# When the first x tile of the layers is loaded: at the start of the kernel, or when the first Gram matrix has been turned

## The chip, the cores and the metric

The kernel runs on one core of one Trainium2 chip. The metric is the time on the device, in microseconds (us), of one execution of the whole program; lower is better. Everything is in 32-bit floats.

## What is computed

x has the shape (16, 32, 128, 128). Two layers follow each other, each as x + layer(group norm of x).

```python
# layer 0: linear attention over channels, 8 images of 32 channels at a time
q = _proj(xf, Wq); kv = _proj(xf, Wkv); k, v = kv[:, :inner], kv[:, inner:]
sim = jnp.einsum('bin,bjn->bij', qh, kh) * scale
attn = jax.nn.softmax(sim, axis=-1)
out = _proj(jnp.einsum('bnj,bjd->bnd', attn, vh), Wout, bout)
# layer 1: windows of 8 x 8, layer norm, then four "fastkan" maps
#   fastkan(t) = exp(-((ln(t) - GRID) / DENOM) ** 2) @ ws.T + silu(t) @ wb.T + bb
z = fastkan1(rows) + fastkan2(columns) + fastkan3(channels)
out = fastkan4(z) + wins
# the whole
x = x + _L0_conv_ref(_gn(x), ...)
x = x + _L1_conv_ref(_gn(x), ...)
```

Layer 0 is linear in x apart from a small matrix that depends on x only through its second moments. The kernel uses this: for each half of the batch (8 images, 256 rows of 16384 values) it forms the 256 x 256 Gram matrix of x, works out from it one small matrix (`pts`) that stands for the normalisation and the attention together, and then applies that matrix to x while layer 1 runs.

## The kernel before

**Two stages.** The first goes once over all of x for the two Gram matrices. The second goes over x again in 64 units (one unit is 128 rows by 1024 columns; two units share one loaded tile `x` of 128 x 2 x 1024 values, 1 MB) and does everything else.

**The Gram stage.** Three tasks pass data along.

- `gram_load` (line 690) fetches x in 16 steps, m = 0 to 15, 2 MB each, eight to a Gram matrix: four DMAs of 256 KB from SP's queue and four from ACT's. The tiles are borrowed from the layers. For m < 8 there are three pairs in turn, (`ad`, `yy`), (`u`, `u`) and (`d`, `sd`); from m = 8 on only the first two, since `d` and `sd` are given back when the first matrix is turned. Step m waits until the last step with its pair has been turned: `"turned", 4 * old[-1] + 3`.
- `gram_turn` (line 711) transposes one block of 512 columns at a time on DVE, four blocks to a step, 32 blocks (`STEPS`) to a matrix, and announces each with `put(("turned", m), None)`. Its two buffers `R` allow it to be two blocks ahead of PE.
- `gram_sum` (line 737) multiplies each turned block with itself on PE and adds up in a PSUM tile `X`.

`attention(bp)` follows each matrix: a long chain of small steps between PE, DVE and ACT that begins with copies of the Gram matrix (the one on ACT is line 799) and ends with `pts[bp]`. `projections` and `parameters` fetch and prepare weights through POOL's queue.

**The first steps of the layers.** `load(n)` (line 1057) fetches `x` for units n and n + 1 with eight DMAs of 128 KB from SP's queue; the pool holds one `x` tile. `layer0_norm(n)` (line 1067) multiplies it with `pts`, so it needs `x` and `attention`. After it come `keep`, `centre`, `rows_norm`, `move`, `norm_a` and the rest of layer 1.

**What sets the order.** Every task is a Python generator that yields steps, each with an engine, an assumed duration and the tiles it takes, or asks for something with `yield "get", key`. A planner (`Flow.run`) runs them against a clock of its own when the program is built, and the order in which it lets steps go is the order of the instructions on each engine. Nothing of its clock reaches the chip; there an instruction waits only for data and for free tiles. The text `ORDER` fixes the order of all named layer tasks on each engine. On SP `load` of unit 0 is the first of them. Until the second Gram matrix is found, only unit 0 holds others back; tasks that are not named, like `gram_load`, fit in where they are not late against a named step that is ready:

```python
late = c[0] > at or (c[0] == at and unit < AHEAD and name not in FIRST)
```

The planner's assumed durations that matter here: `load` 5.2 us of SP; a step of `gram_load` 2.6 us of SP and then 2.6 us of ACT; a sum 0.57 us for a quarter of a block; `parameters` 85 us of POOL, for its many small DMAs.

Of the kernel before, what the change touches and what calls it, by code (L numbers as in the profile page):

```python
# [88 lines left out]
def step(engine, us, *take, lag=None):  # L89


    return engine, us, take, LAG if lag is None else lag


class Flow:
# [22 lines left out]
    def put(self, key, value, late=0.0):  # L118
        self.found[key] = (value, self.now + late)
# [134 lines left out]
def conv_preact_kernel(  # L254
# [248 lines left out]
    def layers():  # L503
        with ExitStack() as es:
# [157 lines left out]
            STEPS = S // 512  # L662
# [385 lines left out]
            def load(n):  # L1048

                if n % 2:  # L1050
                    return
                bp, kk, j = units[n]
                xr, = yield step("SP", 5.2, "x")
                for k in range(KK):
                    for b in range(4):
                        o = slice(32 * b, 32 * b + 32)
                        nc.sync.dma_start(out=xr[o, k, :], in_=x_raw[bp, o, k, j * RB : (j + 1) * RB])
                put(("x", n // 2), xr, fl.moved(2.6, 4.5))
# [509 lines left out]
            with tc.manual_schedule(engines=IN_ORDER):  # L1568
# [25 lines left out]
                        every("assist", assist),  # L1594
                        every("layer0_norm", layer0_norm),
                        every("load", load),
                        every("store", store),
                        ((f"ladder_{k}", n, ladder(k, n)) for k, n in both),
# [85 lines left out]
```

## Time and profile before

| what | value |
|---|---|
| three runs | 2644.55, 2648.94, 2655.05 us; median 2648.94 |
| the profiled execution | 2646.42 us; span in the profile 2644.5 us |
| busy PE, DVE, ACT, POOL | 95%, 93%, 87%, 27% of the span |
| mean granted clock of PE | 0.988 |
| Gram stage: first block turned, first sum of the second matrix, last sum | 17.75, 98.60, about 210.9 us |
| the layers in full swing | from about 244 us |

How to read it: PE is the matrix engine (PEld its weight loads), DVE the vector engine, ACT the scalar engine, SP the engine that mostly issues DMAs. A line of the timeline gives start, length, engine, source line, operation, result <- operand, count, and in brackets the idle time of the engine before it and what ended that. "SPq" and "ACTq" are DMAs being issued; a line with x8 runs from the first issue to the last. A line of windows gives the stretch, its length, the busy time of PE, PEld, DVE, ACT and POOL with the number of instructions, the clock granted to PE (1.00 is full), the mean busy share of the 16 DMA engines, and GB/s (reads and writes as the DMA engines moved them).

### The profile page before, as it was taken

Reading aid. Unit: us, or ns where it says so; the run is one execution under the profiler, and the core shown is the slowest. Engines: PE = TensorE matmul, PEld = TensorE weight load, DVE = VectorE, ACT = ScalarE, POOL = GpSimd, SP = SyncE. Lnnn points to the kernel's source line nnn. Section 1 sums busy time; section 2 is a strip of 40 time slices with the busy share of each in tenths; the row PEclk is TensorE's granted clock in tenths of the full one; section 3 lists DMA queues with packets and bytes.
Section 4 is the critical chain, followed back from the end, with each engine's and each line's share of the span. In section 5 each row is a group of like instructions: output and inputs, shape, how many; then the busy total and the mean of one; then the engine's idle time right before and its main releaser. Section 6 shows DMA issues by size and latency. Waiting matters only on the chain.

```text
span 2644.5 us, 126397 instructions
## 1 busy us (share of the span) xinstructions
PE 2505.3 (95%) x57375; PEld 1300.0 (49%) x57375; DVE 2460.2 (93%) x1697; ACT 2306.0 (87%) x1969; POOL 704.8 (27%) x559
## 2 busy tenths in 40 slices
PE   6998999999999999999999999999999999999875
PEld 6884544444444444444444444444444444444431
DVE  4755899999999999999999999999999999999977
ACT  0007699999999999999999999999999999999973
POOL 4301132232222332232332222322223322323300
PEclk9998999999999999999999999999999999999998
DMA  9752345555555555555555555555555555555521
GB/s 245 193 152 65 106 118 151 147 145 152 144 147 151 155 144 149 145 148 155 145 146 156 139 147 155 153 146 146 147 146 156 142 146 149 146 149 158 140 74 45
DMA packets 306613, 379.86 MB, mean 144 GB/s; under 512 B 42912, under 2 KB 240032, under 8 KB 306080
## 3 DMA queue, kind: packets, MB, share of 16 engines
q1 hardware_dynamic: 292728, 352.22, 48.8%
q10 hardware_dynamic: 9640, 17.11, 2.5%
q8 instruction: 453, 7.42, 1.2%
q0 software_dynamic: 3712, 2.46, 0.4%
q14 instruction: 80, 0.66, 0.1%
HBM read 103.18 MB, written 67.11 MB: 64 GB/s over the span
## 4 chain that ended last, share of the span: by engine, by line
PE 51%; DVE 12%; DMA 10%; ACT 9%; issue 7%; POOL 5%; SPq 5%; DVEq 0%; ACTq 0%; POOLq 0%
PE X L480 25%; DVE u L1276 9%; POOL att L1291 5%; PE X L500 5%; PE Y L1035 4%; DMA out<-xh 4%; PE Y L480 4%; PE X L737 3%; ACT R L1248 3%; PE Y L1213 3%; ACT u L1245 2%; PE Y L1067 2%; ACT z L1389 2%; PE Y L1128 2%; PE X L1477 2%
## 5 line engine op out<-in xcount | busy, mean ns | idle before, releaser
L1276 DVE SCALAR_TENSOR_TENSOR u<-R,u 128x2048 f32<-128x2048 f32 x781 | 1818.4, 2352 | 39.1 <-ACT u L1257 9.7
L480 PE MATMUL X<-u,wt_a 32*32 32x512 f32 x16384 | 666.6, 600 | 12.0 <-ACT u L1257 8.6
L480 PE MATMUL X<-u,wt_b 32*32 32x512 f32 x16896 | 601.4, 600 | 14.3 <-DVE u L1276 12.8
L480 PEld LDWEIGHTS X<-u,wt_a 32*32 32x32 f32 x16384 | 318.1, 103 | 226.2 <-issue 126.3
L1291 POOL TENSOR_SCALAR att<-R 128x1024 f32<-128x1024 f32 x64 | 278.4, 4350 | 548.3 <-ACT R L1248 548.3
L1245 ACT ACTIVATE u<-yc,vec 128x2048 f32<-128x2048 f32 x195 | 391.1, 2006 | 31.0 <-DVE yc L1230 16.1
L1257 ACT ACTIVATE u<-u 128x2048 f32<-128x2048 f32 x195 | 371.0, 1903 | 2.1
L1230 DVE TENSOR_TENSOR yc<-yc,Y 128x1024 f32<-128x1024 f32 x260 | 310.0, 1212 | 18.1 <-PE Y L1213 17.7
L480 PEld LDWEIGHTS X<-u,wt_b 32*32 32x32 f32 x16896 | 206.5, 103 | 237.6 <-issue 104.2
L1320 POOL MEMSET vec<- 128x1 f32 x130 | 12.8, 98 | 1138.9 <-PE X L500 1136.9
L1204 ACT ACTIVATE yc<-Y 128x1024 f32<-128x1024 f32 x260 | 250.0, 1012 | 39.3 <-PE Y L480 38.7
L1248 ACT ACTIVATE R<-yc,vec 128x2048 f32<-128x2048 f32 x130 | 259.6, 1997 | 0.0
L1207 ACT ACTIVATE u<-yc 128x2048 f32<-128x2048 f32 x130 | 247.4, 1904 | 2.2
L1067 PE MATMUL Y<-x,pt 128*128 128x512 f32 x512 | 238.5, 609 | 0.0
L737 PE MATMUL X<-R 128*64 128x193 f32 (+3 forms) x2048 | 153.1, 310 | 24.8 <-DVE R L711 24.3
L1067 PEld LDWEIGHTS Y<-x,pt 128*128 128x128 f32 x512 | 92.9, 191 | 144.4 <-issue 141.0
L737 PEld LDWEIGHTS X<-R 128*64 128x64 f32 x2048 | 142.2, 141 | 39.1 <-DVE R L711 26.3
L1296 POOL TENSOR_TENSOR u<-att,u 128x1024 f32<-128x1024 f32 x64 | 151.9, 2374 | 2.6 <-DVE u L1276 1.4
L1143 POOL TENSOR_SCALAR yy<-yy,vec,col_r 128x1024 f32<-128x1024 f32 x64 | 111.8, 1747 | 147.7 <-DVE yy L1139 125.9
L1366 ACT ACTIVATE ad<-X,col 128x1024 f32<-128x1024 f32 x128 | 135.7, 1120 | 0.8 <-PE X L480 0.6
L500 PE MATMUL X<-sd,ws_a 32*32 32x512 f32 x2048 | 95.8, 598 | 33.3 <-ACT z L1389 18.4
L480 PE MATMUL Y<-yy,c 32*32 32x512 f32 x1056 | 125.2, 598 | 0.4 <-ACT yc L1204 0.4
(222 smaller groups left out, 2929.9 us busy)
## 6 DMA issues: line engine op xcount, KB each, us to landing
xh<-xh SPq DMA_DIRECT2D x512, 128.0 KB
d<-yy SPq DMA_DIRECT2D x512, 128.0 KB
sd<-S SPq DMA_DIRECT2D x512, 128.0 KB
ad_r<-ad SPq DMA_DIRECT2D x512, 128.0 KB
x<-in_x SPq DMA_DIRECT2D x256, 128.0 KB
out<-xh SPq DMA_DIRECT2D x508, 64.0 KB
u<-in_x SPq DMA_DIRECT2D x28, 256.0 KB
u<-in_x ACTq DMA_DIRECT2D x28, 256.0 KB
```

What stands on the lines that cost most here:

```text
L480: MM(dst(to, g_), lhsT=wt[32 * g_ : 32 * g_ + 32, :], rhs=rhs(g_, to ^ cross[g_]), start=start, stop=stop,)
L500: done.append(MM(dst(g_ ^ w, q), lhsT=wt[o, q // 2, :], rhs=rhs(o, q), start=start, stop=stop))
L737: MM(g[64 * q : 64 * q + 64, k, lo:hi], lhsT=t[:, b, at : at + 64], rhs=t[:, b, lo:hi], start=first, stop=last,)
L1067: MM(xp[:, u, :], lhsT=pts[bp][:, k, kk * P : (kk + 1) * P], rhs=xr[:, k, u * 512 : (u + 1) * 512], start=k == 0, stop=k == KK - 1,)
L1204: ACT(v[:, i * RB : (i + 1) * RB], flat(yt[i]), AF.Identity)
L1207: ACT(sq, v, AF.Square)
L1230: TT(v[:, o], v[:, o], flat(rb[i]), ALU.mult)
L1245: ACT(u, v, AF.Square, bias=bqs[k])
L1248: ACT(up, v, AF.Exp, bias=bp_, scale=2.0)
L1257: ACT(u, u, AF.Exp, scale=-1.0, bias=lift)
L1276: STT(t, by, BIG, at, ALU.min, ALU.mult)
L1291: nc.gpsimd.tensor_scalar(rc, by[:, 0:RB], BIG, None, ALU.min)
```

## The change

`load(0)` first asks for `("turned", STEPS - 1)`, the key that `gram_turn` puts when block 31, the last of the first Gram matrix, has been turned. `load` returns at once for odd units, so the one tile concerned is the one for units 0 and 1. No DMA is added, removed or resized, and the loads for later units ask for nothing new.

```diff
                 if n % 2:
                     return
                 bp, kk, j = units[n]
+                if n == 0:
+                    yield "get", ("turned", STEPS - 1)
                 xr, = yield step("SP", 5.2, "x")
                 for k in range(KK):
                     for b in range(4):
```

## The prediction

> **What bounds the kernel now.** The page comes first. After the third of its 40 slices (66 us each) PE, DVE and ACT are all full, and nothing that the change touches lies there. The first slice is the one with a PE of 6 tenths and a DMA of 9.
>
> ```profile
> PE   6998999999999999999999999999999999999875
> PEclk9998999999999999999999999999999999999998
> DMA  9752345555555555555555555555555555555521
> ```
>
> Second, the chain of waits in the first 150 us: start, length, what held.
>
> ```profile
> 0.72 2.65 DMA x<-in_x
> 3.40 6.64 DMA x<-in_x
> 10.05 7.68 DMA ad<-in_x
> 17.75 10.36 DMA u<-in_x
> 28.14 8.25 DMA sd<-in_x
> 36.41 10.78 DMA yy<-in_x
> 47.20 12.93 DMA u<-in_x
> ...
> 61.08 34.80 PE X L737 x358
> ```
>
> Up to 60.3 us only arrivals count, and the first 9.3 us are named x, a tile that nothing reads until much later. From 61.08 the Gram matmuls (L737) carry the chain. Third, the timeline, for the instructions that matter: the x load, the first turned block, the loads of steps m = 8 (ad, yy) and m = 9 (u), the first reader of m = 9, the first reader of x.
>
> ```profile
> 0.72 7.61 SPq L1057 DMA_DIRECT2D x<-in_x  x8
> 17.75 0.71 DVE L711 STREAM_TRANSPOSE R<-ad 128x512 f32<-128x512 f32 x1 [9.17 <-DMA ad<-in_x]
> 61.08 19.20 PE L737 MATMUL X<-R 128*64 128x257 f32 x251 [3.66 <-DVE R L711]
> 87.47 0.42 SPq L690 DMA_DIRECT2D yy<-in_x  x1
> 94.44 2.46 SPq L690 DMA_DIRECT2D u<-in_x  x4
> 94.45 2.48 ACTq L690 DMA_DIRECT2D u<-in_x  x4
> 108.77 1.52 DVE L711 STREAM_TRANSPOSE R<-u 128x512 f32<-128x512 f32 x2 [0.96 <-PE X L737]
> 148.01 3.60 PE L1067 MATMUL Y<-x,pt 128*128 128x512 f32 x8
> ```
>
> Block 36, the first of m = 9, is turned at 108.77 after a wait for PE, not for data. Last, windows, for the room on the DMA engines (the last two columns are the DMA share and GB/s).
>
> ```profile
> 56.00:60.00 4.00, 1.42 (x22) 1.19 (x18) 0.71 (x1) 0.00 (x0) 2.20 (x3) 1.00 1.04 296
> 84.00:86.00 2.00, 2.00 (x33) 1.88 (x31) 1.23 (x3) 0.00 (x0) 2.00 (x5) 1.00 0.08 9
> 94.00:96.00 2.00, 2.00 (x33) 1.88 (x31) 1.23 (x3) 0.00 (x0) 1.67 (x4) 1.00 0.57 145
> 102.00:104.00 2.00, 2.00 (x27) 1.67 (x27) 1.86 (x10) 0.72 (x2) 0.24 (x1) 1.00 0.70 193
> 104.00:106.00 2.00, 2.00 (x21) 1.79 (x17) 1.85 (x11) 0.00 (x0) 0.00 (x0) 1.00 0.03 8
> ```
>
> m = 9 has finished moving by about 103.4 (0.70 of the window that ends at 104), 5.4 us before its reader at 108.77.
>
> **Part 1: x leaves the head of SP's queue.** Eight DMAs of 128 KB, 1.049 MB, and 7.61 us of SP before its first Gram load at 8.38. The DMA engines are saturated (share above 1.0 in every 10 us from 10 to 80), so what is saved is the time of the bytes. Over 4 to 20 us the windows moved 228, 220, 214 and 222 GB/s, mean 221: 1.049 / 0.221 = 4.7 us, by which the first block would be turned earlier. Where the data last holds PE (61.08) the rate is 296 GB/s, because the attention's weights come in beside: 1.049 / 0.296 = 3.5 us. These are the two ends; I take the middle, 4.1 us, since both rates occur on the way.
>
> The Trainium skill ("DMA: Bandwidth & Descriptors", section on bandwidth) gives 341 GB/s for a single 1 MB load issued by GpSimd. By that figure the saving is estimated at 3.1 us. The trace's 221 GB/s, with SP and ACT both loading, disagrees.
>
> Does PE pass it on? In the windows 60 to 100, 100 to 150 and 150 to 211 us it is busy 38.48 + 49.05 + 59.67 = 147.2 of 151 us. This stretch is PE's, so an earlier start shifts its end, and all behind it, by the same amount.
>
> One reserve. PE waits 3.66 us before 61.08, and the clock granted is 0.50 in 62 to 64 and 0.66 in 64 to 66: 2 x 0.50 + 2 x 0.34 = 1.7 us lost. The wait should stay as long as it is, since both its ends move forward by 3.5 to 4.7 us; I change nothing, and keep 1.7 us each way.
>
> The Trainium skill ("TensorE: Matmul & The Clock Gate", Part 1) has the clock halve after an idle window of about 3.4 us that runs freely. By that rule a wait this near the limit may or may not cost its 1.7 us, in either version.
>
> **Part 2: where x lands.** The wait is a "get" of the planner, which only orders the program; the x tile has no earlier user, so the instruction itself should wait for nothing. The planner lets it go when block 31 is turned, the moment at which m = 9 (same block, turn 1) also becomes free. At equal times a named task of unit 0 goes first, so SP's order becomes: m = 8, x, m = 9. On the chip x then starts right behind m = 8, at 87.9 on the old clock, not at 94.4. The gap at 84 to 86 (share 0.08) can't be used, because SP stands in front of m = 8, which waits for its buffer.
>
> Behind x on SP stand four DMAs of m = 9, on which DVE (block 36) and then PE wait. The price: the idle share 0.43 x 2 = 0.9 us of 94 to 96 is filled; the rest of x pushes m = 9. At 260 GB/s (the mean of 96 to 104) x takes 4.0 us, so m = 9 ends at 103.4 + 4.0 - 0.9 = 106.5, still 2.3 us before 108.77. If SP did wait until 94.4, nothing would be filled and m = 9 would end at 107.4, still in time.
>
> ACT's half is reordered too. In the plan SP is taken 5.2 us by x, so ACT's half of m = 9 comes due 5.2 us after block 31, while attention's copy of the Gram matrix (L799) comes due after one more sum, 4 x 0.57 = 2.3 us, and hand-overs, about 3 us. The copy should go first, and it ran at 98.20, waiting for PE: ACT's four DMAs then issue at about 98.5 instead of 94.45. Their 1.05 MB need 4.0 us alone, and SP's share fills the engines before them, so the end stays near 106 to 107. I take 0 for part 2. Its ends are 0 (nothing there waits for less than before, so a gain is excluded) and the whole 4.1 us given back.
>
> x itself is read at 148.01, over 40 us after it lands: no cost. m = 10 is issued at 105.66 and read at 124.10, and takes up the last of the push.
>
> **Part 3: the order around it.** By the planner's costs the Gram starts 5.2 us earlier while "parameters" (85 us on POOL) does not move, so parameter steps slide two blocks later among the Gram's and attention's steps on DVE and PE. No row shows this; the nearest is the one wait of PE for a turned block between 84 and 130 us, 1.5 us long. One such more or less: bounds -1.5 and +1.5, I take 0, because PE is full there with either order. After the second Gram matrix the order is written out for all named tasks, and all of it shifts alike.
>
> **Sum.** -4.1 + 0 + 0 against the profiled execution: its span 2644.5, its time 2646.42, so 2642.3. That execution is 2.5 us below the median of the runs, 2648.94; on the median the forecast is 2644.8.
>
> **Rivals.** *Given back (about 2649).* x costs its 4.1 us in the second Gram instead of the first. For it: x sits right in front of m = 9, and loads there are double, not triple buffered. Against: 5.4 us of slack, and PE sums block 36 only at 113.06. It decides if m = 9 ends after 108.77, which means less than 5.24 MB / 23.1 us = 227 GB/s from 85.64 (two loads and x) on. 96 to 104 ran at 193 to 320.
>
> *Slower (about 2666).* The same lateness, but it repeats: m = 9, 11, 13 and 15 share one buffer, so m = 9 late makes the next of them late, and each late load stops PE as at 57 to 66 us, 3.7 us of wait and 1.7 us of half clock, 5.4 us. All four, 21.6, minus 4.1, give +17.5 on the profiled time, 2663.9, on the median 2666.4; three are not yet past 0.5%. It decides if m = 9 arrives more than about 4.3 us after 108.77, where PE runs out of turned blocks at 113.06, and if nothing makes the delay good. Against: the DMA share is 0.03 in 114 to 116 and 0.01 in 116 to 120, room in which a delay dies out.
>
> *Faster still (about 2639).* The wait before 61.08 and its half clock vanish besides: 4.1 + 3.7 + 1.7 = 9.5 us, on the median 2639.4; only with a run as low as the lowest shown (4.4 below the median) is that past 0.5%. For it, PE's first start gains the larger end; against, a PE that starts earlier waits longer for the same arrival.
>
> **How the numbers follow.** Forecast 0.60, given back 0.16, slower 0.12, faster still 0.12. 0.5% is 13.2 us, about what a measurement of this kernel can tell from no change (its runs span 10.5). The forecast and the given-back case lie within it, and half of faster still: 0.60 + 0.16 + 0.06 = 0.82. Faster is the other half, 0.06, slower 0.12. Range: down, 2644.8 - 1.5 (order) - 1.7 (clock) - 4.4 (lowest run against median) = 2637; up, the given-back 2649 plus 6.1 (highest run against median) = 2655. It leaves out the slower case and the lower half of the faster one.
>
> **What would show it.** Right: the first block turned at 13 to 14 us, the first Gram's last block near 91, x on SP directly behind m = 8 and before m = 9, L799 before ACT's m = 9, no DMA named as what block 36 waited for, and every later stage 3.5 to 4.7 us earlier. Part 2 is wrong if block 36 waits for u; part 1 is wrong if the first block is earlier but PE's second start at 61.08 is not; part 3 is wrong if PE stands idle in the second Gram for more than the 3.8 us of before. A difference that grows along the layers would make the whole argument wrong.

## The result, and the profile after

The changed kernel takes **2667.31 us** (median of 6 runs, 2664.78 to 2673.37) against 2648.47 us (6 runs, 2644.55 to 2657.88) of the kernel before beside it: a ratio of **1.0071, 95% interval 1.0052 to 1.0091**. It is slower by 18.8 us. The forecast was 2644.8 us and no measurable change, so the prediction was wrong. Below, "before" and "after" are the two kernels' profiled executions; the spans are 2644.5 and 2663.0 us, the mean clocks 0.988 and 0.982.

Two rows of the page after, of those that the prediction showed of before:

```profile
PE   7997999999999999999999999999999999999875
PEclk9997999999999999999999999999999999999988
```

PE's first slice rose from 6 to 7 tenths, as wanted: PE starts earlier. Its fourth slice (200 to 266 us) fell from 8 to 7, and the clock there from 8 to 7. From the fifth slice on the row of PE is the same, but a 9 stands for 90% or more and hides a loss of some us. The table below shows that the loss begins in the second Gram matrix and is not complete before the sixth product of the layers, at about 369 us.

The chain of waits after (start, length, what held):

```profile
55.33 10.68 PE X L737 x100
...
177.46 6.15 DMA d<-yy
183.67 6.26 DMA u<-in_x
```

PE's second start, at 61.08 before, is at 55.33. New are two arrivals late in the second Gram matrix, a transfer of `move(0)` (d) and, by the name that the profile gives it, a load of the last Gram step (u).

The timeline after:

```profile
11.04 0.71 DVE L711 STREAM_TRANSPOSE R<-ad 128x512 f32<-128x512 f32 x1 [1.41 <-DMA yy<-in_x]
85.09 12.31 SPq L1059 DMA_DIRECT2D x<-in_x  x8
107.96 0.71 DVE L711 STREAM_TRANSPOSE R<-u 128x512 f32<-128x512 f32 x1 [0.37 <-DMA u<-in_x]
176.12 7.13 SPq L1189 DMA_DIRECT2D d<-yy  x8
183.67 3.21 SPq L690 DMA_DIRECT2D u<-in_x  x4
189.93 2.02 PE L480 MATMUL Y<-d,c 32*32 32x512 f32 x32 [6.07 <-DMA u<-in_x]
198.50 1.52 DVE L711 STREAM_TRANSPOSE R<-u 128x512 f32<-128x512 f32 x2 [2.85 <-PE X L737]
210.42 1.17 PE L1215 MATMUL Y<-lr,back_b 32*128 32x128 f32 x32
215.37 1.21 DVE L1232 TENSOR_TENSOR yc<-yc,Y 128x1024 f32<-128x1024 f32 x1
239.94 1.21 DVE L1232 TENSOR_TENSOR yc<-yc,Y 128x1024 f32<-128x1024 f32 x1
```

And the same places in the timeline of before, which the prediction did not look at:

```profile
181.99 2.54 SPq L690 DMA_DIRECT2D u<-in_x  x4
186.43 8.54 SPq L1187 DMA_DIRECT2D d<-yy  x8
197.69 1.15 PE L480 MATMUL Y<-d,c 32*32 32x512 f32 x32 [1.06 <-DMA d<-yy]
236.87 2.35 DVE L1230 TENSOR_TENSOR yc<-yc,Y 128x1024 f32<-128x1024 f32 x2 [2.85 <-PE Y L1213]
```

The order on SP has turned round. Before, SP issues its half of the last Gram load, m = 15, and then the eight DMAs of `move(0)`. After, `move(0)` comes first (176.12) and the load behind it (183.67), while ACT issues its half of m = 15 at 176.84. And PE, which works in its written order, stands 6.07 us in front of the first products of `norm_a(0)` (L480).

Two things about this stop are easy to misread. First, it is a wait for d, not for m = 15. L480 reads d, and in the trace it waits on the semaphores of the eight DMAs that fill d; the last of these landed at 189.73. The name u comes from a semaphore that a load of u uses again later; in `b_m15late` and `rb_late` below the same stop is named d. The first block of m = 15 was turned at 198.50 after a wait for PE, not for its load. Second, d was not late: before, it landed at 197.35, 7.6 us later. What moved is the place of L480 in PE's order. Before, 60 3/4 of the 64 blocks of the two Gram matrices are summed in front of it, after only 57 1/2 (104 matmuls of L737 stand behind it before and 208 after, 32 to a block). PE comes to it with more of its Gram work still to do, and finds d not yet there.

The last two rows of after show a third place: the two halves of `scale` for norm b of unit 0, one group of two before, are 24.6 us apart. Nothing that the change names lies at any of these places.

How the difference runs along the program (us; "product" is a group of 32 matmuls of L500, the first and second being the first product of the layers with `sd` and with `S`):

| place | before | after | difference |
|---|---|---|---|
| first block turned | 17.75 | 11.04 | -6.7 |
| PE's second start | 61.08 | 55.33 | -5.8 |
| SP issues the first of m = 14 | 172.86 | 166.35 | -6.5 |
| second Gram matrix copied (L799, second time) | 212.09 | 214.53 | +2.4 |
| first product | 240.47 | 246.77 | +6.3 |
| second product | 263.13 | 274.78 | +11.7 |
| sixth product | 353.61 | 369.02 | +15.4 |
| span | 2644.5 | 2663.0 | +18.5 |

Until m = 14 the change is worth 6.5 us. Between m = 14 and the copy of the Gram matrix 8.9 us are lost, then 3.9 more up to the first product, 5.4 up to the second, 3.7 up to the sixth and 3.1 from there to the end. These are single executions, and after's is the fastest of its six: the other kernels below that do the same up to m = 14 issue it at 168.43 to 173.87, so that its 6.5 us may be some us less in others.

### The profile page after: what moved, and what is told of

Its sections match the earlier page's. It is cut to its first block, busy times and chain, and to the rows that moved or that the text cites. A ratio compares the mean times of both kernels' runs of the same rounds, so it can differ in the third digit from the quotient of the medians.

```text
span 2663.0 us, 126402 instructions
## 1 busy us (share of the span) xinstructions
PE 2516.9 (95%) x57375; PEld 1303.7 (49%) x57375; DVE 2458.5 (92%) x1697; ACT 2306.2 (87%) x1969; POOL 700.2 (26%) x559
## 4 chain that ended last, share of the span: by engine, by line
PE 49%; ACT 13%; DMA 11%; DVE 8%; POOL 7%; SPq 6%; issue 5%; ACTq 0%; DVEq 0%; POOLq 0%
PE X L480 25%; POOL att L1293 7%; DVE u L1278 5%; PE X L500 5%; DMA out<-xh 4%; PE Y L1035 4%; ACT R L1250 4%; PE Y L480 4%; ACT u L1247 4%; PE X L737 2%; PE Y L1215 2%; SPq L1550 2%; ACT z L1391 2%; PE X L1479 2%; PE Y L1130 2%
## 5 line engine op out<-in xcount | busy, mean ns | idle before, releaser
L480 PE MATMUL X<-u,wt_a 32*32 32x512 f32 x16384 | 673.7, 605 | 10.8 <-ACT u L1259 8.3
L480 PE MATMUL X<-u,wt_b 32*32 32x512 f32 x16896 | 600.6, 600 | 12.1 <-DVE u L1278 10.6
L480 PEld LDWEIGHTS X<-u,wt_a 32*32 32x32 f32 x16384 | 320.7, 104 | 230.5 <-issue 133.4
L480 PEld LDWEIGHTS X<-u,wt_b 32*32 32x32 f32 x16896 | 207.7, 103 | 232.9 <-issue 99.1
L737 PE MATMUL X<-R 128*64 128x257 f32 (+3 forms) x2048 | 153.7, 309 | 21.9 <-DVE R L711 19.8
L737 PEld LDWEIGHTS X<-R 128*64 128x64 f32 x2048 | 142.7, 141 | 36.8 <-DVE R L711 22.1
L480 PE MATMUL Y<-yy,c 32*32 32x512 f32 x1056 | 126.0, 610 | 2.8 <-DVE att L898 2.4
L500 PE MATMUL X<-sd,ws_a 32*32 32x512 f32 x2048 | 96.9, 605 | 28.5 <-ACT z L1391 19.9
```

What stands on the lines that cost most here:

```text
L480: MM(dst(to, g_), lhsT=wt[32 * g_ : 32 * g_ + 32, :], rhs=rhs(g_, to ^ cross[g_]), start=start, stop=stop,)
L500: done.append(MM(dst(g_ ^ w, q), lhsT=wt[o, q // 2, :], rhs=rhs(o, q), start=start, stop=stop))
L737: MM(g[64 * q : 64 * q + 64, k, lo:hi], lhsT=t[:, b, at : at + 64], rhs=t[:, b, lo:hi], start=first, stop=last,)
```

## The experiments

Theories at the start. *Load 15*: the loss comes from the order of SP, the last Gram load behind `move(0)`. *Place*: it comes from x's DMAs in front of m = 9. *Parameters*: it comes from the parameter steps slid against the others. To tell them apart, the DMAs and the order are taken one without the other.

**The DMAs without the order** (`dma9`). `load(0)` keeps its planned step, and hands its DMAs to `gram_load`:

```diff
+            late = []
             def gram_load():
...
+                    if m == 9:
+                        late[0]()
                     for queue in (nc.sync, nc.scalar):
...
             def load(n):
...
+                if n == 0:
+                    late.append(fetch)    # fetch() issues the eight DMAs
```

> The planner sees the kernel of before, so the order on every engine is that of before; only x's eight DMAs are issued later, on SP directly in front of the loads of m = 9, where the changed kernel has them. Theory 'place' (x's bytes in the second Gram matrix cost the time): about 2667 us, like the changed kernel. Theory 'load 15' (the load of m = 15 fell behind move(0) on SP, and what follows from that order) and theory 'parameters' (attention, Gram and parameter steps interleave otherwise on DVE and PE) both have no cause left here: the 5 to 6 us won at the start remain, less at most 2 us for a late m = 9, so 2642 to 2646 us.

Measured: 2645.68 against 2649.11 us, ratio 0.9982 (0.9965 to 0.9999). First block at 10.96, Gram copied at 206.42, first product at 234.38, 6.1 before that of before. x in front of m = 9 does not cost 19 us: *place* falls.

**The order without the DMAs** (`order`). After, with x issued at the head:

```diff
                 if n == 0:
+                    xr = fl.tile("x")
+                    fetch(xr, bp, j)
                     yield "get", ("turned", STEPS - 1)
+                    fl.give("x")
+                    yield step("SP", 5.2)
+                    del fl.free["x"][0]
```

> The counterpart: the order of the changed kernel on every engine, but x's eight DMAs stay at the head of SP's queue as before. Theory 'place': about 2648 us, like before. Theories 'load 15' and 'parameters': the order costs all it costs and the start wins nothing, so later than the changed kernel by up to the 5 to 6 us of the start: 2668 to 2674 us.

Measured: 2668.26 against 2649.11 us, ratio 1.0077 (1.0052 to 1.0103). From its timeline:

```profile
196.17 2.02 PE L480 MATMUL Y<-d,c 32*32 32x512 f32 x32 [6.19 <-DMA u<-in_x]
```

The whole loss is there, with PE's stop of 6.19 us, though x lies where it lay before. The loss belongs to the order in which the planner lets steps go.

**The last load ahead of `move(0)` again** (`m15`). After, with `move(0)` held in the plan until all sixteen loads are issued:

```diff
             def gram_load():
...
+                put("loaded", None)
...
             def move(n):
+                if n == 0:
+                    yield "get", "loaded"
```

> The changed kernel with one more request: move(0) also waits, in the plan, until all 16 Gram loads have been issued. The parameter steps keep the changed interleaving, the order after the second Gram matrix is that of before again. Theory 'load 15': 2641 to 2646 us, everything lost is back. Theory 'place': 2667 us. Theory 'parameters': 2660 to 2667 us.

Measured: 2650.93 against 2649.11 us, ratio 1.001 (0.9992 to 1.0028). The loss is gone with the parameter steps left as slid, so *parameters* does not carry it by itself. The wait in the plan moved more than SP's two rows, though: PE's order came back with them, with 60 3/4 blocks in front of L480 as before, and its stop at L480 was 0.93 us, so this run can't tell the one order from the other. The 2641 to 2646 us that *load 15* promised were missed: here the wait is at m = 9.

```profile
111.94 1.34 PE L738 MATMUL X<-R 128*64 128x257 f32 x8 [4.95 <-DVE R L712]
```

SP stood 12.06 us on x's DMAs from 86.27, ACT's half of m = 9 went out at 94.22 behind the copy (L799 of after) and SP's at 98.93, and PE stopped 4.95 us.

**The last load planned behind `move(0)`, in before** (`b_m15late`). Before, x at the head, one line in `gram_load`:

```diff
+                        if m == NBP * half - 1:
+                            yield "get", ("d", 0)
                         yield step("SP", 2.6, lag=-2.6)
```

> The kernel of before with one request added: the load of m = 15 waits, in the plan, for move(0). x stays at the head, the parameter steps stay where they were, the order from the end of the second Gram matrix on is that of the changed kernel. Theory 'load 15': 2664 to 2674 us, without any of the change itself. Theories 'place' and 'parameters': 2648 to 2652 us.

Measured: 2670.33 against 2649.11 us, ratio 1.0087 (1.0062 to 1.0112), 21 us without the change.

```profile
192.00 2.02 PE L480 MATMUL Y<-d,c 32*32 32x512 f32 x32 [4.87 <-DMA d<-yy]
```

That is a loss of the same size made by hand. It is not only the stop, though: 4.87 us of PE are not 21. In this kernel too the two halves of `scale` stand apart, at 217.04 and 243.21. And again the one line moved PE's order with SP's: 58 1/2 blocks stand in front of L480 here, and the `rb` step of `norm_b(0)` (L1215 in after) comes ahead of the last Gram block instead of behind it. A load that is planned later moves the end of the Gram stage against unit 0 on every engine. No run has SP's two rows turned round with PE's order kept, or the reverse.

Next, then, *stop* (PE's wait at L480 and what it delays) against *held Y*: `norm_b(0)` takes both PSUM tiles `Y` for its `rb` step (L1215 at 210.42) before the second Gram matrix is found; DVE works in order and comes to the second half of `scale` only at 239.94, so for 25 us attention(1), `layer0_norm` and `rows_norm` share one `Y` instead of two.

**The `rb` step held back** (`rb_late`). After, with one wait in the plan:

```diff
                 give("u")
+                if (name, n) == ("b", 0):
+                    yield "get", ("gram", NBP - 1)
                 rb = yield step("PE", 1.0, "Y", "Y")
```

> The changed kernel with one request added: the step of norm_b(0) that takes both Y tiles waits, in the plan, for the second Gram matrix. m = 15 stays behind move(0), and the stop of PE that belongs to it stays. Theory 'stop': all of the 19 us come from that late load and its stop, 2664 to 2668 us. Theory 'held Y': most of them come from norm_b(0) holding one of the two Y tiles from before the end of the second Gram matrix until a later step of scale_b on DVE, so that attention(1) and the layer steps go through the other one by turns; that part is gone here and the stop remains: 2650 to 2656 us.

Measured: 2652.00 against 2647.43 us, ratio 1.0015 (1.0001 to 1.0029). PE's stop stands, 7.20 us at L480, and the halves of `scale` are together again:

```profile
237.73 2.35 DVE L1234 TENSOR_TENSOR yc<-yc,Y 128x1024 f32<-128x1024 f32 x2 [3.16 <-PE Y L1217]
```

From the copied Gram matrix (216.59) to the first product (242.75) it takes 26.2 us, against 32.2 after and 28.4 before, and from the first to the second 22.05, against 28.01 and 22.66. Stop and earlier start together leave 4.6 of the 18.8 us; the other 14 go with the `rb` step and with what its wait reorders behind it on ACT, DVE, POOL and SP.

**The plan shifted as a whole** (`par80`). If it is the fixed 85 us of `parameters` that keeps the later steps from moving 5.2 us with the Gram stage, then a planned 79.8 us, with no instruction changed, should restore the order:

```diff
-                raw, = yield step("POOL", 85.0, "sz")
+                raw, = yield step("POOL", 79.8, "sz")
```

> The changed kernel with the planner's cost of 'parameters' at 79.8 us, 5.2 less, so that they move with the Gram stage. The order is that of before on all engines, except that x lies in front of m = 9 on SP and attention's copy of the Gram matrix in front of ACT's half of m = 9. Theory 'shifted plan' (the change costs because one task's due time did not move along): 2643 to 2647 us. If ACT's swap matters, m = 9 comes late and PE stops at block 36 for 3 to 5 us as in the kernel with move(0) held behind m = 15: 2648 to 2652 us. Theory 'place': 2667 us.

Measured: 2648.36 against 2647.43 us, ratio 0.9996 (0.9981 to 1.0011). Every engine's order is that of before but for x's place and the copy L799 ahead of ACT's half of m = 9 (60 3/4 blocks again stand in front of L480), and the loss is gone. Gram copied at 208.12, first product 237.35, second 259.31.

**x one load later** (`dma11`). As `dma9`, with `m == 11`: x behind m = 10, where the prediction found the DMA engines empty.

> The order of before on every engine, x's DMAs directly behind the loads of m = 10 instead of in front of m = 9. The DMA engines stand nearly idle there (share 0.03 and less from 114 to 120 us in the profile of before), and m = 9 is not pushed. If x in front of m = 9 cost anything: 2641 to 2644 us, 5 to 7 us under before. If not: 2645 us, like the same kernel with x in front of m = 9.

Measured: 2640.76 against 2647.43 us, ratio 0.998 (0.9967 to 0.9994), faster than both kernels. Block 36 now waits for PE alone, 5.5 us earlier than before:

```profile
103.31 1.52 DVE L714 STREAM_TRANSPOSE R<-u 128x512 f32<-128x512 f32 x2 [0.96 <-PE X L740]
```

**`held Y` by itself** (`scale2`). After, with both halves of `scale` for norm b of unit 0 in one planned step, the orders of PE, SP and POOL unchanged:

```diff
-                    yield step("DVE", 1.14, lag=0.0 if i == 0 else None)
+                    if (name, n, i) != ("b", 0, 1):
+                        yield step("DVE", 1.14, lag=0.0 if i == 0 else None)
```

> The changed kernel with scale_b(0) planned as one step: its second half follows directly after its first on DVE, so that both Y tiles of norm_b(0) come free together. The order on PE, SP and POOL is that of the changed kernel; m = 15 stays behind move(0), and the stop of PE stays. Theory 'held Y': 2650 to 2656 us, as with norm_b(0) held back. Theory 'stop': 2664 to 2668 us; and if it is the earlier place of norm_b(0) on PE rather than the Y tile that costs, also 2664 to 2668 us.

Measured: 2662.24 against 2650.44 us, ratio 1.0042 (1.0025 to 1.0058), between the two expectations.

```profile
195.65 2.02 PE L480 MATMUL Y<-d,c 32*32 32x512 f32 x32 [7.12 <-DMA u<-in_x]
```

Both `Y` tiles are given back at once at 221.06, and from the Gram matrix to the first product it takes 23.4 us instead of 32.2. The held tile is a real cost. But the Gram matrix was copied only at 220.22, and from the first to the second product it still takes 28.3 us as after. That second piece is neither the stop nor the held tile. It goes with the order in which PE and DVE take attention(1) among the first products, which `rb_late` (22.05) and `m15` (22.67) undo and `scale2` does not; that the order is its cause is argued from these runs, not shown by one that changes it alone. In the trace of after PE waits there 2.43 us for DVE (L898) at 267.99, and the mean clock granted to PE over this piece is 0.82 after and in `scale2`, 0.99 to 1.00 in `before`, `rb_late` and `m15`. How much of the 5 us is the wait and how much the clock is not separated.

The clock had a part earlier, too. Two windows over the same stretch, before and then after (PE is busy 36.69 and 32.19 of 45 us, at a clock of 0.85 and 0.70):

```profile
215.00:260.00 45.00, 36.69 (x506) 18.25 (x506) 28.59 (x38) 32.11 (x35) 9.61 (x5) 0.85 0.34 95
215.00:260.00 45.00, 32.19 (x305) 16.02 (x307) 17.36 (x36) 20.95 (x25) 9.57 (x5) 0.70 0.27 75
```

**The place of x and ACT's half of m = 9, on one chip** (`dma9_same`, `par80_same`, `dma11_same`, `dma12`). `dma9` had run on another chip than `par80` and `dma11`. Here they run beside each other, with `dma12`, which has `m == 12`.

> The kernel that keeps the order of before on every engine and issues x's eight DMAs on SP in front of the loads of m = 9, run again on one chip with the next three, since its earlier run and theirs were on different chips. Theory 'place': what is left between these kernels is how late x makes m = 9, so the later x is issued the better. Theory 'swap': x in front of m = 9 costs nothing by itself (block 36 was not late beyond 106.56), and only ACT's half of m = 9 behind the copy L799 costs. 'Place': 0.998 of before, about 3 to 5 us above the kernel with x behind m = 10. 'Swap': within 2 us of it.

> The same order as the run before it except that ACT's half of m = 9 stands behind the copy L799 (parameters planned at 79.8 us). 'Swap': PE again stops 2 to 5 us before the blocks of m = 9, and the time is 2 to 4 us above dma9_same. 'Place': the same time as dma9_same within 1.5 us, since x stands at the same place of SP's queue.

> x's DMAs directly behind the loads of m = 10, order of before otherwise. 'Place': 3 to 5 us below dma9_same, ratio to before 0.9965 to 0.998. 'Swap': within 2 us of dma9_same, 0.998.

> x's DMAs one load later still, directly behind the loads of m = 11, order of before otherwise; the nearest free stretch of the DMA engines. 'Place' and 'swap' both: as dma11_same within 1.5 us, if m = 12 is as little late as m = 11 was; x would be there some 20 us before its first reader. If m = 12 is made late by x and stops PE, 3 to 6 us more than dma11_same.

| kernel | median | ratio to before (2646.45) | 95% interval |
|---|---|---|---|
| `dma9_same` | 2644.83 | 0.9994 | 0.9985 to 1.0004 |
| `par80_same` | 2648.65 | 1.0009 | 0.9997 to 1.0021 |
| `dma11_same` | 2642.49 | 0.9987 | 0.9974 to 1.0000 |
| `dma12` | 2641.89 | 0.9984 | 0.9970 to 0.9999 |

*Swap* is favoured by the times: `par80_same` differs from `dma9_same` in ACT's half of m = 9 behind the copy, and is 3.8 us slower; the means of the twelve runs each are 2648.55 and 2644.46, with standard errors of 1.1. The profiled executions don't show how: PE's longest stop near 105 us is 2.33 us in `par80_same` and 3.40 in `dma9_same` (2.11 in `par80`, 0.32 in `dma9`), so the stop that *swap* expected is not where the 4 us can be seen. *Place* is left with 2.3 us between `dma9_same` and `dma11_same`, less than the 3 to 5 it promised and within the scatter. `dma12` does as `dma11_same`, though SP took 13.93 us to issue x there.

## Why the prediction was wrong, step by step

**Part 1 (x leaves the head): right in kind, the term too small.** 4.1 us were taken, from 3.5 to 4.7; the first block came 6.7 us earlier and PE's second start 5.75. The sum priced x's bytes at 221 to 296 GB/s. SP's first Gram load had also stood behind 7.61 us of issuing x, and the measured saving lies between the price of the bytes and that. The 3.1 us estimated from the Trainium skill's 341 GB/s is further off still.

**Part 2 (where x lands): the order right, the lateness mis-sized.** x went between m = 8 and m = 9 and L799 (92.69) ahead of ACT's half of m = 9 (92.75), as said. But the prediction let x start at 87.9 and m = 9 follow at once, because "the instruction itself should wait for nothing". SP took 12.31 us over x's eight DMAs (85.09 to 97.4), SP's half of m = 9 went out at 99.08, and the second block of m = 9 was named as waiting for u at 107.96. What held SP is told in the last section. The lateness did die out: m = 13 and m = 14 were issued 5.0 and 6.5 us earlier than before. What L799 ahead of ACT's half costs was taken as 0; on one chip the times put it at about 4 us (`par80_same` against `dma9_same`), by a way that the profiles don't show. That would eat most of the gain of part 1, but is not the loss.

**Part 3 (the order around it): the step that failed.** The term was taken as 0 and bounded at 1.5 us each way, "because PE is full there with either order", and the order behind the second Gram matrix was to "shift alike". Neither held. PE was idle 2.3 us in 100 to 211 us before, and 8.8 us in 100 to 215 us after. The 5.2 us by which the plan shifted against a fixed `parameters` did not only slide parameter steps: it brought L480 forward by 3 1/4 blocks, let `move(0)` pass the last Gram load on SP, and let `norm_b(0)` take both `Y` tiles ahead of the last Gram sums. `order` shows that the order alone makes the loss, `dma9` that the DMAs alone do not, and `par80` that the shift against `parameters` is the cause: with no instruction changed it brings the order and the time back. How the planner gets from this shift to these places was not followed. The order of the layers is indeed written out, but relative to each other: `gram_load` and `attention` are not in it and are fitted in anew. The bound itself was read off the wrong row: the 1.5 us is a wait of PE's weight load, and PE's own wait there was 0.63 us.

The loss of after against `dma9`, which has the same x and the old order: 8.1 us at the copied Gram matrix (214.53 against 206.42), which takes in ACT's swap, the stop and the half clock behind it; 4.3 more up to the first product (32.2 us against 28.0), of which `scale2` shows the held `Y` to be the cause; 4.9 more up to the second (28.0 against 23.1), with the order of attention(1) and the lower clock; 4.8 more up to the sixth product, not taken apart. The sum is 22.1, and the medians, each against its own before, are 18.84 + 3.43 = 22.3 us apart; with single executions some us off, the close agreement may be luck.

**Rivals.** *Slower* had the size, +17.5, by another road, which is luck: four late loads in one buffer from m = 9 on. In the trace no load of m = 11 to 15 stopped PE; the one long stop is for d. Its remark that the room at 114 to 120 us lets a delay die out was right. *Given back* is what `par80` measures, with the order out of the way. *Faster still* is what `dma11` and `dma12` come nearest to in time, without reaching 2639, but its mechanism did not occur: PE's wait before its second start was 3.66 us before, 3.30 after and 3.68 in `dma11`.

**Signs.** The prediction had named the right one: "part 3 is wrong if PE stands idle in the second Gram for more than the 3.8 us of before". The 3.8 us are of 60 to 211 us; after, PE stood 6.07 us at once. The sign for part 2 came in part: block 36 was turned at 106.89 after 2.38 us with no DMA named, but block 37, at 107.96, waited for u. The first block was turned at 11.04, earlier than the 13 to 14 us that were to show part 1 right. And "a difference that grows along the layers", which was to make the whole argument wrong, is what the table shows, from +6.3 at the first product to +18.5 at the end, though 15.4 of the 18.5 are there by the sixth product. A window of after shows what the DMA engines did during the stop (last two columns: share and GB/s):

```profile
184.00:186.00 2.00, 0.00 (x0) 0.00 (x0) 0.23 (x1) 0.00 (x0) 0.00 (x0) 1.00 1.09 204
```

PE is empty, the engines are full, with `move(0)` from SP and m = 15 from ACT and SP beside each other. The Trainium skill ("DMA: Bandwidth & Descriptors", section "Issuing engines are not separate DMA queues") says that DMAs from several issuers share the same 16 engines; this window agrees, with 204 GB/s at a share of 1.09 for the three issues together. It adds that the time to initiate a DMA is usually small beside the DMA. Each of x's eight issues took SP 0.31 to 0.43 us after, which agrees; the rest of the 12.31 us was waiting, as the last section shows.

A stop costs more than itself. Behind the 6.07 us the clock granted to PE was 0.51 over 190 to 196 us, against 1.00 over 197 to 203 before. The first 32 matmuls of L480 took 2.02 us, against 1.15 for the same group before, which came after a wait of 1.06 us, and the next 32 sums of L737 took 4.37 against 2.41: 2.8 us more on top of the stop. In `b_m15late` the group of L480 took 2.02 too, after 4.87. The Trainium skill ("TensorE: Matmul & The Clock Gate", Part 1) puts the idle window that halves the clock at about 3.4 us; 6.07 and 4.87 us did it here, and both agree.

## What to carry to other kernels

In a kernel whose order comes from a plan, a wait put into the plan is an edit to every in-order queue behind it, not to one DMA: before pricing it, list the order of each engine and queue with and without it, and count, for each product that waits for a transfer, how much independent work still stands in front of it. Here 3 1/4 blocks less of it left PE standing for a transfer that came earlier than before. To move a transfer alone, keep its planned step and issue its DMAs elsewhere, at a place where the trace shows the DMA engines empty; here that gave 0.1 to 0.2% (`dma11`, two runs), the plan's way cost 0.7%. And a reordering that looks free because an engine is full must be looked at for how long it holds a shared tile: two halves of one step torn apart kept one of two PSUM tiles for 25 us. When a profile names what ended a wait, look at what the waiting instruction reads: here the name was that of another transfer on the same semaphore.

## What the runs showed of the hardware that was not expected

SP stood on the eight DMAs of x far longer than issuing them takes, with no tile to wait for. The waits of SP's queue after, between 84 and 110 us (total, times, longest):

```profile
SPq L1059 <- DMA yy<-in_x: 5.9, 2, 3.5
SPq L1059 <- DMA u<-in_x: 3.2, 1, 3.2
SPq L1059 <- DMA ad<-in_x: 2.6, 1, 2.6
```

L1059 issues x, and its tile has no earlier user, yet these waits come to 11.7 of the 12.31 us. The trace shows what they are for: SP and ACT share eight semaphores, which their DMAs signal in turn, and each issue first waits for the semaphore that it will use itself, which is free once an earlier DMA on it has landed. So this is the program's own bookkeeping and not a limit of the queue, and an instruction here waits for a third thing besides data and free tiles. Eight DMAs of 128 KB took SP 3.58 us where their semaphores were free (`rb_late` at 220.21), 6.05 us at 104.90 in `dma11`, 11.14 us in `dma9`, 12.31 us after and 13.93 us in `dma12`. Whatever stands behind them on the queue is late by that, before any byte of it moves.

Open are the 4.8 us up to the sixth product, how the 5 us between the first and second product divide between waits and clock, and how `par80_same` comes to be slower than `dma9_same`.
